# Attention's product sets: the closing product in its own PSUM bank, added by DVE, and the first feed-forward block's weights in a buffer of their own

## The chip, the core and the metric

The kernel runs on one core of a Trainium2 chip. The core has five engines that run their own instruction streams in order and meet through semaphores: TensorE (PE: matmuls, with its weight loads listed as PEld), VectorE (DVE), ScalarE (ACT), GpSimd (POOL) and SyncE (SP, which here issues nearly all DMAs). Matmul results land in PSUM, here in tiles of one bank (128 x 512 float32); everything else lives in SBUF, which DMAs fill from and store to HBM. The metric is the device time of one execution in microseconds, lower is better.

## The reference

One pre-norm transformer block over x of shape 2048 x 1024, all in float32, cut to what matters:

```python
def attn(h):                    # h = layernorm(x); 32 heads of 32
    q, k, v = (h @ w.T + b for w, b in ((wq, bq), (wk, bk), (wv, bv)))
    # per token: the 32 heads attend to one another, not to other tokens
    s = einsum('bshd,bstd->bsht', q, k) / sqrt(32)
    return einsum('bsht,bstd->bshd', softmax(s), v)

def ffn(h):                     # h = layernorm(x); 2752 hidden units
    dq1, dq2, dq3 = (nf4_quant_dequant(w) for w in (w1, w2, w3))
    return (silu(h @ dq1.T) * (h @ dq2.T)) @ dq3.T

x = x + attn(layernorm(x))
x = x + ffn(layernorm(x))
```

`nf4_quant_dequant` takes blocks of 64 weights, divides each by its largest magnitude, replaces every value by the nearest of 16 codes and multiplies back. The kernel does this on the chip, so each weight matrix has to pass through DVE and ACT before it can be used.

## The kernel before, in words

**Products.** Large matrix products are done by a Strassen-Winograd scheme: two 2 x 2 block matrices are multiplied with 7 block products in place of 8. For attention, a *product set* takes a pair of 128-token tiles (the four quadrants A11, A12, A21, A22 of their transposed activations and the sums S1 to S4) against a 1024 x 1024 projection held in SBUF as blocks B11, B21, B22 and differences T1 to T4. `products` (L314 to L358) issues the seven: SA11·B11, S3·T3, S2·T2, SA12·B21, S1·T1, S4·B22, SA22·T4, each four matmuls of 128 x 128 by 128 x 512 (`mm4`; the profile shows each as two instructions, hence x8 a product). They accumulate in place: bank `z` takes B11, T2, T1 and B22 one after the other, and ACT copies its value out in between (`g0`, `u2`, `u4`, L329) before PE may add the next; bank `q` takes T3 and T4; SA12·B21 has a bank `r` from a rotating pair (tag `x`), which also serves transposes of background weights (`ptw`) and of normalized rows (`pt` in `keep_T`). The four quadrants of the result are put together in `ce` and `co`: three by DVE adds (L346, L350, L356), the last by an ACT copy of `z` after S4·B22 (L353).

**Sweeps.** There are three sweeps of eight sets: q, k and v (in this order). Between products `products` calls `fill(n)`, n naming the product that follows in the author's count: 7, 6, 2, 5, 3, 4. A sweep's `fill` puts other work there:
- q: PE transposes of the next pair's normalized rows (`Inputs.transposes`), which ACT copies into `A` and, for v, into `V`; DVE then makes S1 to S4 (`differences`) and stores them for later sweeps.
- k: `part()`, a half of one tile's scores on PE (128 small matmuls by the profile's count), whose softmax is done by DVE and ACT. The scores of a tile take a PSUM tile `at` of four banks, of which there is one.
- v: `part()`, a half of one tile's context; DVE then transposes it (L620), adds the residual, stores it (`x1d`) and normalizes the row in place. `keep_T` transposes normalized rows on PE and stores them, and for every second tile makes four differences `xU` on DVE and stores those, as operands of the feed-forward products.

**Background.** All along, a generator `background` quantizes the feed-forward weights, 65 jobs in a fixed order. A job is an absmax, 15 steps (ACT scales into `sg`, L211, of which there are two buffers; DVE clamps and accumulates into `r`, L216) and a rescale. `advance(n)` issues n such steps; `flush(n)` moves the finished job's PE transposes (`ptw`) and ACT copies on. In the sweeps `fill` calls both; in the feed-forward loop `spent(us)` calls `advance` at 0.67 steps per microsecond of PE work issued.

**Order.** PE's instructions stand in the order in which the source issues them. Those of the other engines are placed by a scheduler that knows their dependences, so a step on DVE or a DMA on SP can stand earlier or later than its source line; on the chip each engine then runs its list strictly in order.

**First block.** After the v sweep the pools of the sweeps are closed. `plain_block` (L764) multiplies the first chunk of feed-forward weights without the Winograd scheme, eight products of four matmuls, with the last halves of context and `keep_T` in between. Its weights come by `load_w12(0, plain=True)` (L732), into a tile of the pool `wT`, which takes the SBUF space of the closed pool `pair`. Then units of seven products (`Unit`) and down projections (`down`) follow to the end: the feed-forward loop.

Of the kernel before, what the change touches and what calls it, by code (L numbers as in the profile page):

```python
# [58 lines left out]
def preln_block_kernel(  # L59
# [192 lines left out]
    wpool = ctx.enter_context(tc.tile_pool(name="op", bufs=1, side="left"))  # L252
    pair = left.enter_context(tc.tile_pool(name="pair", bufs=1, side="left"))
# [5 lines left out]
    SA11, SA12, SA22, S1, S2, S3, S4, SA21 = range(8)  # L259
# [60 lines left out]
    def products(A, fill, used=lambda name: None):  # L320
# [13 lines left out]
        g0 = copied("g0", z)  # L334
        q = ps_pj.tile([P, TB], FP, tag="q", name="q")
# [12 lines left out]
        mul(z, S1, "T1", False, False)  # L348
# [3 lines left out]
        mul(z, S4, "B22", False, True)  # L352
        nc.scalar.copy(ce[:, 512:], z)  # L353
# [6 lines left out]
    def differences(t):  # L360

        nc.vector.tensor_tensor(t[:, S1], t[:, SA21], t[:, SA22], ALU.add)
        nc.vector.tensor_tensor(t[:, S2], t[:, S1], t[:, SA11], ALU.subtract)
        nc.vector.tensor_tensor(t[:, S3], t[:, SA11], t[:, SA21], ALU.subtract)  # L364
        nc.vector.tensor_tensor(t[:, S4], t[:, SA12], t[:, S2], ALU.subtract)
# [60 lines left out]
    class Inputs:  # L426
# [3 lines left out]
        def __init__(self, p):  # L430
            self.p = p
            self.xn = [normed_x(2 * p + j) for j in range(2)]
            self.A = pair.tile([P, 8, 4, P], FP, tag="A", name="A", bufs=2)
            self.V = work.tile([P, 8, 4, P], FP, tag="AV", name="AV")

        def transposes(self, j):
            for half in range(2):
                pt = ps_t.tile([P, 4, P], FP, tag="pt", name="pt")
                for k in range(4):
                    nc.tensor.transpose(pt[:, k, :], self.xn[j][:, ts(4 * half + k, P)], ident)  # L440
                n = (SA11, SA12, SA21, SA22)[2 * j + half]
                nc.scalar.copy(self.A[:, n], pt)
                nc.scalar.copy(
                    self.V[:, n].rearrange("p k (c m) -> p k c m", c=4),
# [3 lines left out]
        def finished(self):  # L448
            differences(self.A)
            nc.sync.dma_start(opD[self.p], self.A[:, 0:7])  # L450

        def finished_v(self):
            differences(self.V)
            nc.sync.dma_start(opV[self.p], self.V[:, 0:7])
# [39 lines left out]
    def load_A(src, p):  # L494
        t = pair.tile([P, 8, 4, P], FP, tag="A", name="A", bufs=2)
        nc.sync.dma_start(t[:, 0:7], src[p])
        return t

    for p in range(NP):
# [7 lines left out]
        def fill(n):  # L507
            if n in (7, 3):
# [82 lines left out]
    for p in range(NP):  # L591
# [3 lines left out]
        def fill(n):  # L595
# [3 lines left out]
            if n in (3, 5):  # L599
# [55 lines left out]
    def keep_T(i, x1n):  # L655
# [18 lines left out]
        for n in range(4):  # L674
            u[n + 1] = work.tile([P, 4, P], FP, tag="xU", name="xU", bufs=3)
# [4 lines left out]
    for p in range(NP):  # L680
        nextA = load_A(opV, p + 1) if p + 1 < NP else None
        i = 2 * p - 4

        def fill(n):
            if n in (7, 2, 5, 4) and (p, n) != (1, 7):
                part()
            advance(2 if n == 6 else 1)
            if n in (7, 4):
                flush(1)
            if n == 5 and i in x1n:  # L690
                keep_T(i, x1n.pop(i))
            if n == 3:
                if p == 0:
                    part()
                elif i + 1 in x1n:
                    keep_T(i + 1, x1n.pop(i + 1))
# [334 lines left out]
```

## Time and profile before

| what | value |
|---|---|
| median of 3 runs | 2572.02 us (2563.67 to 2575.69) |
| profiled execution, its own time | 2561.21 us |
| profiled execution, span | 2559.4 us |
| PE busy | 2438.9 us (95%) |
| DVE busy | 2020.1 us (79%) |
| ACT busy | 1673.7 us (65%) |
| POOL busy | 31.7 us (1%) |
| mean granted PE clock | 0.985 |
| DMA | 506 MB, 198 GB/s |

Starts of product sets in the profiled execution (us): q 13.1, 44.7, 71.6, 103.3, 135.4, 166.0, 192.7, 223.8; k 250.8, 278.4, 317.0, 351.4, 381.6, 411.5, 447.2, 477.7; v 512.4, 546.2, 577.8, 610.1, 649.8, 686.6, 720.0, 757.0. The first block's products start at 801.9, the first unit's at 842.4. Sets are numbered 1 to 24 in this order.

How to read it: a busy time is that of an engine's own instructions, with neither waits nor DMA issues in it. Matmuls overlap their neighbours, so PE's busy time includes pipelining. The granted clock is what the power throttle let PE have; at 0.5 a matmul takes twice as long. Windows give these numbers for a stretch of time; waits list the idle time of an engine before an instruction, with what released it.

### The profile page before, as it was taken

How to read it: one execution, taken by the hardware profiler on the slowest of the kernel's cores; microseconds unless marked ns; L12 is line 12 of the kernel's file. 1: busy time of each engine (PE TensorE's matmuls, PEld its weight loads, DVE VectorE, ACT ScalarE, POOL GpSimd, SP SyncE). 2: the span in 40 equal slices, each digit the busy share in tenths (PEclk: the TensorE clock that was granted, in tenths of full speed). 3: DMA queues.
4: the chain of work that ended last, by engine and by line, in shares of the span. 5: the costliest groups of instructions: out<-in, count | busy, mean ns of one | idle time of the engine just before them, and what ended most of it. 6: DMA issues, size and time to landing. Idle time of an engine off the chain costs nothing.

```text
span 2559.4 us, 36651 instructions
## 1 busy us (share of the span) xinstructions
PE 2438.9 (95%) x14160; PEld 1134.1 (44%) x14160; DVE 2020.1 (79%) x2240; ACT 1673.7 (65%) x3190; POOL 31.7 (1%) x72
## 2 busy tenths in 40 slices
PE   8899899999998999999999999999999999999998
PEld 4444444444444444444444444444444444444433
DVE  8999798888998588888888888889888897871222
ACT  4656554444654478979888898888987978861000
POOL 1000000000000000000000000000000000000000
PEclk9999999999999999999999999999999999999999
DMA  8778543656668673354644547335365253641474
GB/s 301 286 281 335 210 162 121 233 189 221 224 218 290 218 271 144 136 212 138 263 155 135 198 149 265 149 118 215 128 251 192 107 205 136 234 176 70 142 279 150
DMA packets 156848, 506.03 MB, mean 198 GB/s; under 512 B 13632, under 2 KB 67904, under 8 KB 136832
## 3 DMA queue, kind: packets, MB, share of 16 engines
q1 hardware_dynamic: 156096, 503.63, 54.3%
q8 instruction: 111, 1.82, 0.3%
q14 instruction: 65, 0.53, 0.1%
q10 hardware_dynamic: 576, 0.05, 0.0%
HBM read 317.77 MB, written 185.86 MB: 197 GB/s over the span
## 4 chain that ended last, share of the span: by engine, by line
PE 22%; DVE 21%; ACT 18%; issue 6%; DMA 1%; DVEq 0%; SPq 0%
DVE r L216 17%; PE z L311 9%; PE po L929 7%; ACT sg L211 7%; ACT wn L172 6%; PE q L311 3%; ACT r L172 3%; PE rr L311 2%; ACT wop L147 1%; DVE acc L950 1%; DMA acc<-x1d 1%; PE po L941 1%; DVE r L214 1%; DVE r L227 1%; PE ptw L146 0%
## 5 line engine op out<-in xcount | busy, mean ns | idle before, releaser
L211 ACT ACTIVATE sg<-wn 128x1024 f32<-128x1024 f32 (+1 forms) x975 | 1011.0, 1047 | 318.9 <-DVE r L216 272.4
L216 DVE SCALAR_TENSOR_TENSOR r<-sg,r 128x1024 f32<-128x1024 f32 (+1 forms) x910 | 1103.1, 1212 | 111.9 <-ACT sg L211 73.9
L929 PE MATMUL po<-w,h 128*128 128x512 f32 x1344 | 595.1, 597 | 17.0 <-DVE acc L950 13.8
L929 PEld LDWEIGHTS po<-w,h 128*128 128x128 f32 x1344 | 250.0, 190 | 336.5 <-issue 286.8
L311 PE MATMUL z<-xB,w 128*128 128x512 f32 x720 | 322.7, 597 | 13.7 <-DMA w<-wd 11.3
L311 PE MATMUL z<-xT,w 128*128 128x512 f32 x656 | 297.2, 596 | 2.0 <-ACT u L861 1.9
L311 PE MATMUL q<-xT,w 128*128 128x512 f32 x656 | 291.0, 592 | 0.0
L172 ACT ACTIVATE wn<-wn,rc 128x64 f32<-128x64 f32 x1032 | 270.1, 335 | 26.4 <-DVE rc L192 26.4
L311 PEld LDWEIGHTS z<-xB,w 128*128 128x128 f32 x720 | 134.5, 191 | 174.5 <-issue 164.3
L311 PE MATMUL z<-wB,A 128*128 128x512 f32 x384 | 188.6, 637 | 22.4 <-ACT u L329 22.4
L950 DVE TENSOR_TENSOR acc<-acc,po 128x512 f32<-128x512 f32 x192 | 129.7, 681 | 101.6 <-PE po L929 58.4
L311 PEld LDWEIGHTS q<-xT,w 128*128 128x128 f32 x656 | 123.6, 190 | 151.4 <-issue 149.5
L311 PE MATMUL z<-wT,A 128*128 128x512 f32 x384 | 181.3, 616 | 8.4 <-ACT u L329 6.4
L311 PEld LDWEIGHTS z<-xT,w 128*128 128x128 f32 x656 | 122.9, 191 | 149.8 <-issue 140.7
L311 PE MATMUL q<-wT,A 128*128 128x512 f32 x384 | 173.1, 593 | 3.0 <-DVE A L364 2.0
L172 ACT ACTIVATE r<-r,am 128x64 f32<-128x64 f32 x608 | 152.4, 338 | 27.9 <-DVE r L216 27.8
L311 PE MATMUL rr<-xB,w 128*128 128x512 f32 x328 | 150.0, 600 | 0.0
L184 DVE TENSOR_REDUCE am<-wn 128x16 f32<-128x1024 f32 (+1 forms) x65 | 78.3, 1204 | 59.4 <-ACT r L172 55.5
L311 PEld LDWEIGHTS z<-wB,A 128*128 128x128 f32 x384 | 75.0, 205 | 106.5 <-issue 79.3
L311 PEld LDWEIGHTS z<-wT,A 128*128 128x128 f32 x384 | 72.1, 195 | 91.0 <-issue 81.2
L311 PEld LDWEIGHTS q<-wT,A 128*128 128x128 f32 x384 | 71.8, 190 | 90.9 <-issue 84.2
L861 ACT COPY u<-z 128x512 f32<-128x512 f32 x41 | 23.5, 573 | 131.6 <-PE z L311 131.6
(104 smaller groups left out, 1798.4 us busy)
## 6 DMA issues: line engine op xcount, KB each, us to landing
w<-wd SPq DMA_DIRECT2D x41, 1280.0 KB, 6.9
acc<-x1d SPq DMA_DIRECT2D x96, 512.0 KB, 3.8
wd<-wop SPq DMA_DIRECT2D x21, 2048.0 KB, 7.0
x1d<-acc SPq DMA_DIRECT2D x80, 512.0 KB, 2.9
wn<-in_w_dram SPq DMA_DIRECT2D x63, 512.0 KB, 4.0
w<-wd SPq DMA_DIRECT2D x62, 512.0 KB, 4.1
xT<-xdT SPq DMA_DIRECT2D x28, 1024.0 KB, 7.2
xB<-xdB SPq DMA_DIRECT2D x24, 1024.0 KB, 5.2
```

The costliest lines, as they stand in the source:

```text
L147: nc.scalar.copy(o[:q, first + half], pt[:q])
L172: nc.scalar.mul(dst[:, ts(n, BLOCK)], src[:, ts(n, BLOCK)], by[:, n : n + 1])
L184: nc.vector.tensor_reduce(am[:, :nb], v.rearrange("p (b e) -> p b e", e=BLOCK), AX.X, ALU.max, apply_absolute_value=True,)
L211: nc.scalar.activation(t, v, AF.Copy, bias=EDGES[i], scale=BIG)
L214: nc.vector.tensor_scalar(r, t, code, -1.0, ALU.min, ALU.max)
L216: nc.vector.scalar_tensor_tensor(r, t, code, r, ALU.min, ALU.max)
L227: nc.vector.tensor_tensor(r3, r3, f, ALU.mult)
L311: nc.tensor.matmul(dst, w[:, k, :], xop[:, k, :], start=start and k == 0, stop=stop and k == 3, skip_group_check=True,)
L861: nc.scalar.copy(u2, self.z)
L929: nc.tensor.matmul(po, hs[c][j][:, ts(q, P)], w3T[c][:, ts(n, 512)], start=(c == g[0]), stop=(c == g[-1]), skip_group_check=True,)
L941: nc.tensor.matmul(po, hs[NFULL][r, ts(q, P)], w3T[NFULL][r, ts(n, 512)], start=False, stop=True, skip_group_check=True,)
L950: nc.vector.tensor_tensor(a[:, ts(n, 512)], a[:, ts(n, 512)], po, ALU.add)
```

## The change

- `products`: S1·T1 now closes the accumulation in `z`. S4·B22 goes into a bank of its own, `r3`, from the rotating pair, and the last quadrant of `ce` is the DVE add of `u4` and `r3` in place of the ACT copy of `z`. There is one more call of `fill`, with n = 1, after the first product.
- `fill` in the three sweeps: the points at which `flush`, `advance`, `keep_T` and `part` run are moved; in q and k the new call issues one background step more, in v it issues none, n = 6 issues one in place of two, and three follow the set in place of two.
- The quadrant A21 leaves the tiles `A` and `V` (seven blocks of 2 KB a partition in place of eight) and gets tiles of its own for q and v; `xU` has two buffers in place of three.
- The space so freed holds a pool `w0` of 8 KB a partition, made before the sweeps' pools. The first block's weights are loaded there by an instruction that the source places at the start of the last v set, and `plain_block` is handed the tile.

```diff
--- before.py
+++ after.py
@@ -250,13 +250,15 @@
 
 
     wpool = ctx.enter_context(tc.tile_pool(name="op", bufs=1, side="left"))
+    w0p = ctx.enter_context(tc.tile_pool(name="w0", bufs=1, side="left"))
     pair = left.enter_context(tc.tile_pool(name="pair", bufs=1, side="left"))
     ps_pj = left.enter_context(tc.tile_pool(name="ps_pj", bufs=1, space=PSUM, side="left"))
     small = right.enter_context(tc.tile_pool(name="small", bufs=2, side="right"))
     ctx.enter_context(tc.manual_schedule(engines={nc.tensor.engine}))
 
     NP = NT // 2
-    SA11, SA12, SA22, S1, S2, S3, S4, SA21 = range(8)
+    SA11, SA12, SA22, S1, S2, S3, S4 = range(7)
+    SA21 = -1
     qD = [tc.dram_tile([P, 32, NH], FP, name=f"qD{i}") for i in range(NT)]
     pD = [tc.dram_tile([P, 32, NH], FP, name=f"pD{i}") for i in range(NT)]
     opD = [tc.dram_tile([P, 7, 4, P], FP, name=f"opD{p}") for p in range(NP)]
@@ -332,6 +334,7 @@
         z = ps_pj.tile([P, TB], FP, tag="z", name="z")
         mul(z, SA11, "B11", True, False)
         g0 = copied("g0", z)
+        fill(1)
         q = ps_pj.tile([P, TB], FP, tag="q", name="q")
         mul(q, S3, "T3", True, False)
         s7 = copied("s7", q)
@@ -345,23 +348,24 @@
         co = pair.tile([P, E], FP, tag="C1", name="co")
         nc.vector.tensor_tensor(ce[:, 0:512], g0, r, ALU.add)
         fill(2)
-        mul(z, S1, "T1", False, False)
+        mul(z, S1, "T1", False, True)
         u4 = copied("u4", z)
         nc.vector.tensor_tensor(co[:, 512:], u4, s7, ALU.add)
         fill(5)
-        mul(z, S4, "B22", False, True)
-        nc.scalar.copy(ce[:, 512:], z)
+        r = bank("r3")
+        mul(r, S4, "B22", True, True)
+        nc.vector.tensor_tensor(ce[:, 512:], u4, r, ALU.add)
         fill(3)
         mul(q, SA22, "T4", False, True)
         nc.vector.tensor_tensor(co[:, 0:512], u2, q, ALU.add)
         fill(4)
         return ce, co
 
-    def differences(t):
-
-        nc.vector.tensor_tensor(t[:, S1], t[:, SA21], t[:, SA22], ALU.add)
+    def differences(t, a21):
+
+        nc.vector.tensor_tensor(t[:, S1], a21, t[:, SA22], ALU.add)
         nc.vector.tensor_tensor(t[:, S2], t[:, S1], t[:, SA11], ALU.subtract)
-        nc.vector.tensor_tensor(t[:, S3], t[:, SA11], t[:, SA21], ALU.subtract)
+        nc.vector.tensor_tensor(t[:, S3], t[:, SA11], a21, ALU.subtract)
         nc.vector.tensor_tensor(t[:, S4], t[:, SA12], t[:, S2], ALU.subtract)
 
     def qk_T(t, c, b):
@@ -430,8 +434,10 @@
         def __init__(self, p):
             self.p = p
             self.xn = [normed_x(2 * p + j) for j in range(2)]
-            self.A = pair.tile([P, 8, 4, P], FP, tag="A", name="A", bufs=2)
-            self.V = work.tile([P, 8, 4, P], FP, tag="AV", name="AV")
+            self.A = pair.tile([P, 7, 4, P], FP, tag="A", name="A", bufs=2)
+            self.V = work.tile([P, 7, 4, P], FP, tag="AV", name="AV")
+            self.a21 = work.tile([P, 4, P], FP, tag="A21", name="A21")
+            self.v21 = work.tile([P, 4, P], FP, tag="V21", name="V21")
 
         def transposes(self, j):
             for half in range(2):
@@ -439,19 +445,20 @@
                 for k in range(4):
                     nc.tensor.transpose(pt[:, k, :], self.xn[j][:, ts(4 * half + k, P)], ident)
                 n = (SA11, SA12, SA21, SA22)[2 * j + half]
-                nc.scalar.copy(self.A[:, n], pt)
+                a, v = (self.a21, self.v21) if n == SA21 else (self.A[:, n], self.V[:, n])
+                nc.scalar.copy(a, pt)
                 nc.scalar.copy(
-                    self.V[:, n].rearrange("p k (c m) -> p k c m", c=4),
+                    v.rearrange("p k (c m) -> p k c m", c=4),
                     pt.rearrange("p k (m c) -> p k c m", c=4),
                 )
 
         def finished(self):
-            differences(self.A)
-            nc.sync.dma_start(opD[self.p], self.A[:, 0:7])
+            differences(self.A, self.a21)
+            nc.sync.dma_start(opD[self.p], self.A)
 
         def finished_v(self):
-            differences(self.V)
-            nc.sync.dma_start(opV[self.p], self.V[:, 0:7])
+            differences(self.V, self.v21)
+            nc.sync.dma_start(opV[self.p], self.V)
 
     load_x(0)
     load_x(1)
@@ -492,8 +499,8 @@
         return lambda name: load_W(m, name)
 
     def load_A(src, p):
-        t = pair.tile([P, 8, 4, P], FP, tag="A", name="A", bufs=2)
-        nc.sync.dma_start(t[:, 0:7], src[p])
+        t = pair.tile([P, 7, 4, P], FP, tag="A", name="A", bufs=2)
+        nc.sync.dma_start(t, src[p])
         return t
 
     for p in range(NP):
@@ -505,7 +512,7 @@
             nxt = Inputs(p + 1)
 
         def fill(n):
-            if n in (7, 3):
+            if n in (1, 6):
                 flush(1)
             if n == 5 and more:
                 nxt.transposes(0)
@@ -596,7 +603,7 @@
             if n in (7, 2, 5, 4):
                 part()
             advance(1)
-            if n in (3, 5):
+            if n in (1, 6):
                 flush(1)
 
         cs = products(A, fill, (lambda name: None) if p + 1 < NP else next_W("v"))
@@ -672,28 +679,33 @@
         b12, b22 = t[:, 0], t[:, 1]
         u = {}
         for n in range(4):
-            u[n + 1] = work.tile([P, 4, P], FP, tag="xU", name="xU", bufs=3)
+            u[n + 1] = work.tile([P, 4, P], FP, tag="xU", name="xU", bufs=2)
             y, z = ((b12, b11), (b22, u.get(1)), (b22, b12), (b21, u.get(2)))[n]
             nc.vector.tensor_tensor(u[n + 1], y, z, ALU.subtract)
             nc.sync.dma_start(xd[f"T{n + 1}", tbp][:, :, cols], u[n + 1])
 
     for p in range(NP):
-        nextA = load_A(opV, p + 1) if p + 1 < NP else None
+        if p + 1 < NP:
+            nextA = load_A(opV, p + 1)
+        else:
+
+            until("2", 0)
+            nextA = w0p.tile([P, 4, 4, P], FP, tag="w0", name="w0")
+            nc.sync.dma_start(nextA, wd["2", 0][:, 0:4])
         i = 2 * p - 4
 
         def fill(n):
             if n in (7, 2, 5, 4) and (p, n) != (1, 7):
                 part()
-            advance(2 if n == 6 else 1)
-            if n in (7, 4):
+            advance(0 if n == 1 else 1)
+            if n in (1, 2):
                 flush(1)
-            if n == 5 and i in x1n:
+            if n == 7 and i in x1n:
                 keep_T(i, x1n.pop(i))
-            if n == 3:
-                if p == 0:
-                    part()
-                elif i + 1 in x1n:
-                    keep_T(i + 1, x1n.pop(i + 1))
+            if n == 3 and p == 0:
+                part()
+            if n == 4 and i + 1 in x1n:
+                keep_T(i + 1, x1n.pop(i + 1))
 
         cs = products(A, fill, (lambda name: None) if p + 1 < NP else next_op)
         flush(1)
@@ -708,7 +720,7 @@
             t = work.tile([P, 32, D], FP, tag="vd", name="vd", bufs=3)
             v_T(t, cs[j], vb_sb)
             parts.append(gather(2 * p + j, pl[j], t))
-        advance(2)
+        advance(3)
         A = nextA
     hook["scale"] = "DVE"
     left.close()
@@ -729,14 +741,11 @@
             load_op(name, tbp)
         return ops[tag][2]
 
-    def load_w12(c, plain=False):
+    def load_w12(c):
         until("2", c)
         t = wT.tile([P, 7, 4, P], FP, tag="w12", name="w12")
-        if plain:
-            nc.sync.dma_start(t[:, 0:4], wd["2", c][:, 0:4])
-        else:
-            nc.sync.dma_start(t[:, 0:2], wd["2", c][:, 0:2])
-            nc.sync.dma_start(t[:, 2:7], wd["2", c][:, 3:8])
+        nc.sync.dma_start(t[:, 0:2], wd["2", c][:, 0:2])
+        nc.sync.dma_start(t[:, 2:7], wd["2", c][:, 3:8])
         return t
 
     def load_w3(c):
@@ -761,9 +770,8 @@
     def new_h():
         return hp.tile([P, TB], FP, tag="h", name="h", bufs=10)
 
-    def plain_block(c, tbp):
-
-        w = load_w12(c, plain=True)
+    def plain_block(w, tbp):
+
         hs = []
         for j in range(2):
             zs = []
@@ -789,7 +797,7 @@
 
 
 
-    plain = plain_block(0, 0)
+    plain = plain_block(A, 0)
     i = NT - 4
     next(plain)
     next(plain)
```

## The prediction

> **What bounds the kernel now.** I read the page's engine totals first, then one row for each stage, single product sets, then who waits for whom, and last the timeline at the places of the edits. Windows: stretch, length, then PE, PEld, DVE, ACT and POOL busy, PE's granted clock, DMA share, GB/s. The rows are the q sweep, the k sweep, seven v sets, the eighth v set with the first feed-forward block, and the feed-forward loop:
>
> ```profile
> 13.10:250.80 237.70, 217.12 (x585) 101.64 (x585) 222.89 (x281) 143.28 (x292) 16.44 (x28) 0.97 0.80 300
> 250.80:512.40 261.60, 241.58 (x4059) 120.68 (x4057) 225.15 (x221) 133.29 (x250) 0.00 (x0) 0.97 0.50 186
> 512.40:757.00 244.60, 226.20 (x3963) 117.72 (x3960) 216.85 (x227) 133.07 (x271) 8.16 (x22) 0.97 0.62 209
> 757.00:842.40 85.40, 72.91 (x1340) 39.39 (x1329) 69.12 (x77) 35.30 (x69) 4.56 (x10) 0.94 0.83 278
> 842.40:2559.40 1717.00, 1673.90 (x4202) 747.93 (x4200) 1281.66 (x1429) 1225.12 (x2305) 0.00 (x0) 0.99 0.49 179
> ```
>
> From 842 on PE is busy 1674 of 1717 us at clock 0.99: that loop is PE's. Before it (829 us) PE and DVE share the work nearly evenly, and which one ends a set changes from set to set. Four whole sets, k 14 and 15, v 22 and 23:
>
> ```profile
> 411.50:447.20 35.70, 31.26 (x581) 15.63 (x569) 35.08 (x33) 21.02 (x35) 0.00 (x0) 0.95 0.37 130
> 447.20:477.70 30.50, 30.50 (x581) 15.72 (x577) 23.16 (x26) 10.89 (x26) 0.00 (x0) 1.00 0.34 129
> 686.60:720.00 33.40, 32.43 (x604) 17.54 (x594) 25.99 (x31) 13.70 (x43) 1.48 (x4) 1.00 0.72 238
> 720.00:757.00 37.00, 33.30 (x586) 17.14 (x584) 35.61 (x36) 24.42 (x42) 1.49 (x4) 0.95 0.59 197
> ```
>
> The quantization job of the background moves in lumps: a set that holds 11 to 15 of its steps (L216) is full on DVE and lasts 35 to 37 us with PE at clock 0.95; a set with 1 is PE's, 30.5 us in k and 33.4 us in v, while DVE idles 7 us. ACT is half idle throughout, so what ACT loses is worth nothing by itself. Who waits in these 829 us (total, times, longest), and the places:
>
> ```profile
> ACT sg L211 <- DVE r L216: 113.4, 123, 6.1
> PE z L311 <- ACT u L329: 28.8, 14, 4.3
> PE z L311 <- DMA w<-wd: 11.3, 1, 11.3
> PE sc L390 <- DVE kd L382: 5.6, 1, 5.6
> ...
> 746.18 5.40 PE L311 MATMUL z<-wB,A 128*128 128x512 f32 x8 [2.96 <-ACT u L329]
> ...
> 752.29 3.60 PE L311 MATMUL q<-wT,A 128*128 128x512 f32 x8
> ...
> 801.88 8.89 PE L311 MATMUL z<-xB,w 128*128 128x512 f32 x16 [11.30 <-DMA w<-wd]
> ```
>
> `z<-wB` after an ACT wait is the closing product S4·B22, held by the copy of u4 out of the same bank. The copy is late because ACT's queue stands behind `sg`, which waits for DVE: the wait is DVE's in the end.
>
> **Part 1, the bank of its own.** Of the 28.8 us, 22.4 stand in the row of `z<-wB`: 2.8, 2.7 and 1.8 in q, 3.3 at k's first set, 4.3, 2.9 and 3.0 in v, the rest below 1. The stall also costs clock: 5.40 us where a product takes 3.60, so 1.8 more at five of them. Gross 22.4 + 5 x 1.8 = 31 us of PE time. *Trainium skill, "TensorE: Matmul & The Clock Gate", Part 1: the clock falls after an idle window of about 3.4 us. By that the 2.96 us stall would cost no clock and the gross would be 22 us; the row shows that it does cost it, so I keep 31.*
>
> Against it: the ACT copy of `ce` (0.59 us, 24 times) becomes a DVE add. Its nearest row is L346, 0.68 us, the same shapes with one side in PSUM; but what DVE pays is the distance from start to start:
>
> ```profile
> 758.48 0.70 DVE L677 TENSOR_TENSOR xU<-xT 128x512 f32<-128x512 f32 x1
> 759.08 0.69 DVE L356 TENSOR_TENSOR co<-u,q 128x512 f32<-128x512 f32 x1
> ...
> 734.45 1.21 DVE L216 SCALAR_TENSOR_TENSOR r<-sg,r 128x1024 f32<-128x1024 f32 x1
> 735.58 1.20 DVE L624 TENSOR_TENSOR x<-x,cx 128x1024 f32<-128x1024 f32 x1
> ```
>
> 0.60 us an add, 1.13 us a background step. So +4.8 us of DVE in each sweep. *"Perfetto Trace Analysis", Optimizing Scalar/DVE Operations, says to hand work from a saturated DVE to Scalar; this edit does the reverse. By it all 14.4 us would be paid; by the rows only those in sets that DVE ends.* In the new DVE order the add stands after the next context's transpose and residual add (3.0 us), which fits under the closing product (3.4 us), so the bank comes free in time for the transposes that reuse it; if DVE is over 5 us late, PE waits there instead.
>
> **Part 2, the calls of `fill`.** There are seven now. q and k issue one step more a set; v still nine. Counted in the built order of DVE, steps done at the end of q, k, v and at the second h of the first block: 58, 119, 180, 195 before; 59, 134, 195, 208 after. So q +1, k +14, v 0, block -2. They leave the feed-forward loop, where PE ends everything, for sweeps where DVE often does.
>
> *q.* DVE 222.9 of 237.7: its bound. +1 x 1.13 + 4.8 = 5.9 us; the three stalls removed let DVE's idle time shrink by at most what stands beside them (0.75, 0.75, 1.9 = 3.4). Bounds 0 to +6, taken +2.5.
>
> *k.* 14 x 1.13 + 4.8 = 20.6 us. Cover: set 10 (278 to 317), where DVE idles 12.0 us, in two waits of 3.9 and 5.3, while PE waits for `kd`; in the new order 18 steps stand there, not 4. That leaves 8.6. The three light sets with idle DVE (3.9, 7.9, 7.1) could take it, but the new order keeps lumps of 14, 1, 12, 3, 14, so I give them half: +4. The stalls of the other k sets stand at the scores (`sc`), whose single PSUM tile waits for softmax on DVE, and stay. Bounds -3 (all hidden, and the 3.3 us stall gone) to +12 (only the idle of set 10 used).
>
> *v.* The new order has 9 and 6 steps in turn in place of 14, 1, 15. At 34.3 us of DVE work (its instructions by the distances above) and 33.4 us, PE's pace in the row of set 22, I take 35 and 33.4: sets 20 to 23 last 136.8, not 147.0 (39.7 + 36.9 + 33.4 + 37.0): -10. Set 24 had no step and gets nine: +3.5. Sets 17 to 19 keep a lump of 15: 0. Sum -6.5, taken -7 for the clock. `xU` has two buffers, not three: the third difference now waits for the store of the first (median 4.3 us from issue to landing) with 0.6 to 2 us of other work between; some 2.3 us of DVE a set, hidden in the 6-step sets, and queued behind it is the transpose that frees the context tile for PE. Bounds -18 (all at PE's pace) to +4.
>
> **Part 3, the weights of the first block.** No wait holds the new load, and in SP's built order it stands back in the q sweep, so the 11.3 us and 8.89 - 6.9 = 2 us of clock go. What is late next is DVE. It had covered that wait with 14 steps (795 to 814); these now lie among the block's residual chains. From the last `co` add to the last normalized row DVE has 38 us of work by the same distances, plus about 4 us for the third `xU` (four differences in a row) and 4 to 5 for `h`, which waits for PE's fourth half-product: 47 to 48 us against 51.5 (790.1 to 841.6). -3; bounds -12 (PE alone: its products, contexts and transposes take 40.5) to +5.
>
> **Feed-forward.** Both orders start a new job after the first unit's h, the new one a job ahead. Nothing is gained while PE ends the loop; but three transposes waited 11.7 us for jobs, with slow clock after (some 6.8 us more). A job ahead may remove one or shift them: -10 to +5, taken -3.
>
> **Sum.** 2.5 + 4 - 7 - 3 - 3 = -6.5 us on the profiled execution: span 2559.4, time 2561.2, to 2555. The median of the runs lies 10.8 above it, 2572.0; I give 2565.
>
> **Rivals.** *A, DVE pays (slower):* the new order holds 27.8 us more DVE work before the loop (5.9 + 20.6 + 4.8, less the block's 2 steps and smaller moves). If DVE's idle time doesn't shrink except in set 10 (12 us), 16 are paid, and with `xU` holding v at its old pace the block's gain is lost: 2588. For it: heavy sets idle DVE under 1.5 us; against: the v lumps go. It decides once the even v sets last 36 us or more. *B, PE's pace is reached (faster):* v -18, block -8, loop -8, q and k 0: 2538. For it: 31 + 13 us of PE stalls go; against: DVE set most of them. *C, the load was hidden anyway:* DVE's steps under the wait were work that had to be done, the block keeps its 51.5 us and the waits move to context and h: 2572 with part 1's small sums.
>
> **How the numbers follow.** 0.5%, 12.9 us, is about what a measurement of this kernel can tell from no change. The forecast with C (2559 to 2580): 0.40; B and what lies towards it: 0.34; A: 0.26. A few of the first group's cases fall past the near bound, so faster 0.38, same 0.34, slower 0.28. The forecast's own range is 2553 to 2580; with both rivals cut at one in ten, 2540 to 2591.
>
> **What would show it.** Right: no PE wait for `u` before a closing product; v sets 20 to 23 at 33 to 36 us; k longer by a few us; no wait on the load, with PE's next waits at context on the transpose behind `xU`. Wrong: v sets still at 37 (A), or the stretch from 13 to the first unit shorter by over 20 us (B).

## The result, and the profile after

The changed kernel takes 2591.02 us (median of 4 runs, 2588.82 to 2595.1) against 2570.73 us before (4 runs on the same chip, 2563.67 to 2575.69). The ratio is 1.0087, with a 95% interval of 1.0069 to 1.0106: slower by 20 us, where 7 us faster was forecast. The profiled execution went from 2561.21 to 2591.23 us, its span from 2559.4 to 2589.4. That is 30 us, since the profiled execution of before lies 9.5 below the median beside it and that of the changed kernel 0.2 above its own. So the stages below add up to 10 us more than the medians differ by.

The windows of the changed kernel, stage by stage as before (q, k, seven v sets, the eighth with the first block, the loop), and then v sets 20 to 23. Columns: stretch, length, busy time of PE, PEld, DVE, ACT and POOL, PE's granted clock, DMA share, GB/s:

```profile
12.69:248.70 236.01, 214.31 (x586) 99.99 (x585) 225.52 (x288) 138.87 (x285) 13.72 (x28) 0.98 0.80 300
248.70:524.10 275.40, 246.44 (x4065) 123.07 (x4063) 250.54 (x249) 151.09 (x291) 0.00 (x0) 0.94 0.51 188
524.10:770.70 246.60, 225.19 (x3972) 117.07 (x3961) 209.21 (x221) 116.46 (x238) 11.33 (x20) 0.97 0.60 204
770.70:867.90 97.20, 77.97 (x1331) 42.49 (x1330) 79.37 (x88) 42.44 (x70) 7.95 (x12) 0.90 0.79 266
867.90:2589.40 1721.50, 1676.91 (x4193) 747.56 (x4192) 1266.22 (x1414) 1207.76 (x2280) 0.00 (x0) 1.00 0.49 176
624.20:664.30 40.10, 33.76 (x587) 17.36 (x586) 35.74 (x40) 18.15 (x37) 3.44 (x5) 0.91 0.66 205
664.30:697.90 33.60, 32.38 (x594) 17.27 (x593) 26.51 (x29) 14.60 (x30) 1.48 (x4) 1.00 0.69 229
697.90:736.10 38.20, 33.38 (x587) 17.21 (x586) 33.84 (x39) 17.80 (x36) 3.04 (x5) 0.96 0.64 201
736.10:770.70 34.60, 32.45 (x594) 17.33 (x593) 27.02 (x29) 15.00 (x32) 1.90 (x4) 1.00 0.62 214
```

Against the rows of before: q 1.7 us shorter, k 13.8 longer, the seven v sets 2.0 longer, the last set with the block 11.8 longer, the loop 4.5 longer. DVE's work ahead of the loop rose from 734.0 to 764.6 us (the sum of its four rows), and the loop starts 25.5 us later. The loop got 15.4 us less of DVE work and no shorter for it. In set 22 DVE has 33.8 us of work, as the prediction counted (34.3), yet the set lasts 38.2 and DVE idles 4.4 of them. So its pace is not DVE's alone.

Who waits, in the first 870 us of the changed kernel (total, times, longest):

```profile
ACT xT L669 <- DVE xU L684: 23.2, 7, 6.6
PE r L313 <- ACT xT L669: 19.3, 5, 6.3
DVE xU L684 <- DMA xdT<-xU: 16.0, 6, 6.2
...
PE sc L394 <- DMA ql<-qD: 11.9, 1, 11.9
...
PE ptw L146 <- ACT r L172: 8.2, 1, 8.2
...
PE pt L668 <- DVE x L308: 6.3, 1, 6.3
...
PE z L313 <- ACT u L331: 3.8, 5, 1.5
```

PE's wait for `u` fell from 28.8 us to 3.8, and the 11.3 us for the first block's weights are gone. In their place PE waits 19.3 us for a bank that ACT has to empty into `xT` first. The timeline of set 22 (start, length, engine and line, what ended the idle time before it) shows who holds whom:

```profile
706.11 1.09 PE L668 MATMUL pt<-ident,x 128*128 128x128 f32 x8
707.03 3.60 PE L313 MATMUL z<-wT,A 128*128 128x512 f32 x8
...
712.29 1.92 DVE L627 STREAM_TRANSPOSE cx<-cx 128x1024 f32<-128x1024 f32 x1
714.07 0.67 DVE L684 TENSOR_TENSOR xU<-xT,xU 128x512 f32<-128x512 f32 x1
...
714.81 1.07 ACT L669 COPY xT<-pt 128x512 f32<-128x512 f32 x2 [1.35 <-DVE xU L684]
...
715.45 5.40 PE L313 MATMUL r<-wB,A 128*128 128x512 f32 x8 [4.82 <-ACT xT L669]
```

`keep_T`, moved to n = 7, transposes into the rotating pair at 706.1. The product that takes the pair next is not the closing S4·B22 but SA12·B21, one product later. ACT may not copy `pt` into `xT` until DVE has made the last difference `xU` that reads the old `xT`, and that stands behind steps and a context transpose. PE idles 4.82 us, and SA12·B21 then takes 5.40 us in place of 3.60. The same wait stands in sets 20 and 24 (6.34 and 4.78 us).

### The profile page after: what moved, and what is told of

Same layout as the page of the kernel before. It is cut to its first block, busy times and chain, and to the rows that moved or that the text cites. A ratio compares the mean times of both kernels' runs of the same rounds, so it can differ in the third digit from the quotient of the medians.

```text
span 2589.4 us, 36654 instructions
## 1 busy us (share of the span) xinstructions
PE 2447.9 (95%) x14160; PEld 1136.9 (44%) x14160; DVE 2035.3 (79%) x2264; ACT 1660.2 (64%) x3166; POOL 35.5 (1%) x72
## 4 chain that ended last, share of the span: by engine, by line
DVE 23%; ACT 21%; PE 16%; issue 7%; DMA 2%; DVEq 0%; SPq 0%
DVE r L216 18%; ACT sg L211 8%; ACT wn L172 6%; PE po L937 6%; PE z L313 5%; ACT r L172 4%; PE q L313 3%; ACT wop L147 1%; PE rr L313 1%; DVE acc L958 1%; DVE am L184 1%; DVE r L227 0%; DVE r L214 0%; ACT g L873 0%; DMA acc<-x1d 0%
## 5 line engine op out<-in xcount | busy, mean ns | idle before, releaser
L313 PE MATMUL r<-wB,A 128*128 128x512 f32 x384 | 188.1, 636 | 19.3 <-ACT xT L669 19.3
L147 ACT COPY wop<-ptw 128x512 f32<-128x512 f32 (+1 forms) x130 | 74.6, 574 | 77.1 <-PE ptw L146 77.0
L313 PEld LDWEIGHTS r<-wB,A 128*128 128x128 f32 x384 | 75.7, 204 | 109.9 <-issue 85.0
```

The source lines that it names most:

```text
L147: nc.scalar.copy(o[:q, first + half], pt[:q])
L313: nc.tensor.matmul(dst, w[:, k, :], xop[:, k, :], start=start and k == 0, stop=stop and k == 3, skip_group_check=True,)
```

## The experiments

The differences below are between ratios to the kernel before, in units of 2572 us; their margins join the two runs' intervals. First the kernel was cut into its parts.

**Part 3 alone.** The kernel before with the `w0` pool, A21 in tiles of its own, `xU` with two buffers; products and `fill` as before.

```diff
+    w0p = ctx.enter_context(tc.tile_pool(name="w0", bufs=1, side="left"))
...
+            nextA = w0p.tile([P, 4, 4, P], FP, tag="w0", name="w0")
+            nc.sync.dma_start(nextA, wd["2", 0][:, 0:4])
```

> The kernel before with part 3 alone: the first block's weights in a buffer of their own, A21 in tiles of its own, two xU buffers; products, fill and steps as before. Forecast's step for part 3 (-3 us): ratio 0.997 to 1.000, the wait of 11.3 us gone. Theory X (two buffers cost more than the wait gave): the block's waits on the xU stores come with it, ratio 1.000 to 1.005. Theory S says only that it is not slower: 0.995 to 1.000.

2562.23 us, 0.9965 (0.9953 to 0.9977): 9 us faster than before. The window of its last v set and first block, 97.2 us in the changed kernel:

```profile
761.60:844.70 83.10, 75.07 (x1340) 40.51 (x1329) 68.55 (x77) 34.87 (x68) 4.70 (x10) 0.94 0.88 294
```

The row of before had 85.4. Its profiled execution (2565.9) lies above its median, that of before below, so the rest of the 9 us cannot be placed in the two traces. What the rest of the change costs is 0.0122, 31 us. All further single edits stand on this kernel, called the base here.

**Three xU buffers on the base** (room from single `mx` and `sm` tiles of the softmax).

> The kernel before with the weights' own buffer and three xU buffers (room from single buffers for the softmax's maxima and sums). If the store of the first difference holds DVE as it does in the changed kernel: 0.993 to 0.996, 2552 to 2560 us, the eighth v set some 3 to 5 us shorter than its 34.0 or the block shorter than its 49.1. If the third buffer is worth nothing here: 0.996 to 0.998.

2562.53 us, 0.9975 (0.9961 to 0.9989): no gain.

**The bank alone, and DVE's copy alone.** The first puts S4·B22 into `r3` with DVE's add, with `fill` as before; the second keeps the product set of before and lets DVE copy `z` in ACT's place.

```diff
-        nc.scalar.copy(ce[:, 512:], z)
+        nc.vector.tensor_copy(ce[:, 512:], z)
```

> The kernel before with the weights' own buffer, and with the bank r3 and DVE's add; fill is called as before (six times, no n = 1). Theory P1: 1.005 to 1.011, 2583 to 2598 us, and PE waits some 15 us or more before S4*B22 in r for ACT's copies. Theory P2: 0.990 to 0.998, 2545 to 2565 us: the 22 us of waits for u before the closing product go and nothing takes their place. If the two parts only cost together (the moved transposes of keep_T meet the shared bank): both this run and the one with fill alone below 1.000.

> The kernel before with the weights' own buffer, and the copy of z after S4*B22 on DVE instead of ACT: 24 more DVE instructions of about 0.6 us, 14.4 us, and no new bank. If DVE's share of the work is what makes the bank variant slow: 1.000 to 1.004, 2570 to 2581 us (8 to 18 us over the buffer alone at 0.9965). If DVE's idle time takes them: 0.995 to 0.998, 2557 to 2566 us; then the DVE add is no part of the loss.

2578.2 us, 1.0021 (1.0008 to 1.0035), and 2575.11 us, 1.0016 (1.0005 to 1.0027). Handing 24 instructions of 0.6 us from ACT to DVE costs 0.0051, 13 us (9 to 17), nearly all of their 14.4. The bank as a whole costs 14, 1 us more than DVE's copy alone (-3 to 6), so taking the closing product out of `z` bought nothing that can be told. PE's waits before 870 us, on the base and then with the bank on it:

```profile
PE z L313 <- ACT u L331: 27.1, 16, 4.3
```

```profile
PE r L313 <- ACT xT L668: 18.4, 5, 6.7
...
PE q L313 <- DVE co L359: 8.6, 5, 3.8
```

Here `keep_T` stands at n = 5, just ahead of S4·B22, and it is that product that waits in the rotating pair, 18.4 us. Another 8.6 us (0.3 on the base) stand before S3·T3 of the next set, whose bank `q` DVE's last add `co` still has to read. Together that is the base's 27.1 us for `u`. By stages, one execution each, the bank made q shorter (229.1 us, 233.1 on the base), k longer (276.1, 270.5) and the seven v sets, where `keep_T` runs, longer by 14 (259.7, 245.6).

**The moved calls without the bank.** The changed kernel with the product set of before, `fill(1)` kept.

> The changed kernel with the product set of before: S4*B22 accumulates in z again and ACT copies it out; the calls of fill (n = 1 among them) stay where the change put them, and so does the weights' own buffer. Reference point: the buffer alone with the fill of before measured 0.9965 of before, the whole change 1.0087, some 31 us apart. Theory P1 (the bank r3 and DVE's add cost it): 0.994 to 0.999, 2555 to 2568 us, no PE wait for xT copies before S4*B22. Theory P2 (the new fill points cost it): 1.005 to 1.011, 2583 to 2598 us, with the k sweep at 270 us or more and the eighth v set with the first block at 95 us or more. If each part costs something of its own: 0.999 to 1.005.

2589.7 us, 1.0078 (1.0059 to 1.0098): 0.0113, 29 us, over the base. This part does nearly the whole damage; the bank on top of it adds 2 us (-5 to 9), which cannot be told from nothing. Its last v set and block take 95.8 us, close to the changed kernel's 97.2; its k takes 268.0, no more than the base, with all the added steps in it.

**The moved calls one at a time, on the base.** `flush` at its new points; `keep_T` at n = 7 and 4 in v; one step more a set in q and k; v's ninth step from n = 6 to the end of the set.

```diff
+        fill(1)
...
-            if n == 5 and i in x1n:
+            if n == 7 and i in x1n:
...
-            advance(2 if n == 6 else 1)
+            advance(0 if n == 1 else 2 if n == 6 else 1)
```

> The kernel before with the weights' own buffer (0.9965 of before) and, of the moved calls, only flush: at n = 1 and 6 in q and k, at 1 and 2 in v; no step at n = 1, keep_T and the steps as before. All the moved calls together, without the bank, measured 1.0078: some 29 us. Theory F (the rotating pair is taken by a job's transposes just before SA12*B21 needs it, and jobs end at other places): 1.002 to 1.008, 2576 to 2590 us, with PE waits in the rows of r or ptw. If flush's place is worth nothing: 0.994 to 0.999, 2555 to 2568 us.

> The kernel before with the weights' own buffer and, of the moved calls, only v's keep_T, at n = 7 and 4 in place of 5 and 3. Theory K (keep_T at n = 7 puts its two pt tiles into the rotating pair one product ahead of SA12*B21, which then waits for ACT's copies, themselves held by the xU that reads the old xT): 1.001 to 1.006, 2574 to 2587 us, PE r behind xT copies 15 us or more in v, the eighth v set 5 us longer than its 34.0. If the move is harmless alone: 0.994 to 0.999.

> The kernel before with the weights' own buffer and, of the moved calls, only one background step more a set in q and k (n = 1), so that one whole job of 15 steps leaves the feed-forward loop for the sweeps. Theory S (steps are free in the loop and paid in the sweeps): 15 x 1.13 = 17 us more DVE work before the loop, 1.001 to 1.004, 2574 to 2582 us, the first unit 8 us or more later than at 844.7. If DVE's idle time takes them, as taking them out of the whole change suggested: 0.994 to 0.999.

> The kernel before with the weights' own buffer and, of the moved calls, only v's ninth step: after the set (three there) in place of a second one at n = 6. No step count changes. Theory V (where the lumps of a job fall against the sets decides it, and this moves them): more than 6 us either way from 0.9965, so under 0.994 or over 0.999. If the place of one step is worth nothing: 0.994 to 0.999.

| on the base | median us | ratio to before | against the base |
|---|---|---|---|
| flush moved | 2568.05 | 0.9989 (0.9977 to 1.0002) | +6 us (2 to 10) |
| keep_T moved | 2578.93 | 1.0032 (1.0018 to 1.0046) | +17 us (13 to 22) |
| steps added | 2587.59 | 1.0059 (1.0037 to 1.0080) | +24 us (18 to 31) |
| ninth step moved | 2563.86 | 0.9965 (0.9951 to 0.9979) | 0 us (-5 to 5) |

What `flush` costs stands in the first block. On the base the job that runs there makes its first step (L214) 4 us after the block's first product, with `flush` moved 22 us after it. The rows are the base's, then those with `flush` moved:

```profile
799.78 0.68 DVE L214 TENSOR_SCALAR r<-sg 128x1024 f32<-128x1024 f32 x1
```

```profile
812.91 0.68 DVE L214 TENSOR_SCALAR r<-sg 128x1024 f32<-128x1024 f32 x1
...
844.53 1.94 PE L667 MATMUL pt<-ident,x 128*128 128x128 f32 x8 [7.31 <-DVE x L308]
```

DVE idles early in the block, then has the steps in front of the last normalized row, and PE waits 7.31 us for that row. From its first product to the first unit the block takes 55.1 us, on the base 49.1. The other traces agree: in all nine kernels with `flush` at its new points the block takes 52.5 to 55.2 us and PE's wait for that row 5.3 to 10.5; in the ten others with the parts of the change, 45.5 to 50.0, and the wait is 3.4 at most.

With `keep_T` moved, PE waits at SA12·B21, as in the changed kernel:

```profile
PE r L313 <- ACT xT L667: 15.3, 5, 7.1
```

Added steps cost more than their DVE work (15 x 1.13 = 17 us). Set 10 shows where some of it stands. Its window in the kernel with added steps, and PE's largest wait in it:

```profile
281.60:331.10 49.50, 34.08 (x570) 16.81 (x568) 43.15 (x42) 35.90 (x76) 0.00 (x0) 0.83 0.48 178
```

```profile
PE sc L393 <- DVE kd L385: 12.4, 1, 12.4
```

The set holds 20 steps and lasts 49.5 us, where the base's has 6 and lasts 42.7. DVE's former idle time there is used, but PE stands still beside it, here until DVE has made `kd`. That wait is mostly not new. On the base PE waits 10.1 us at the same place for `ql`. So the wait accounts for some 2 of the 6.8 us.

**Steps taken out, and added elsewhere.** Without the step at n = 1 in q and k: from the whole change, and from the moved calls without the bank. The bank on the base with it. And the base with a step less a set (none at n = 6 in q and k).

```diff
-            advance(0 if n == 5 else 1)
+            advance(0 if n in (5, 1) else 1)
```

> The changed kernel, but the new call of fill issues no background step in q and k, so that these sweeps hold as many steps as in the kernel before. Theory S (steps: the k sweep's +13.9 us is DVE work of 14 background steps that the feed-forward loop did for nothing): k falls from 275 to 260-264 us, v and the first block stay at 247 and 97 +-4, the total is 10 to 16 us below the changed kernel, ratio to before 1.002 to 1.005. Theory X (the two xU buffers and the earlier keep_T hold ACT and PE in v and in the block, and k's growth is the adds' and the late ql load's): k falls by 5 us at most, ratio 1.006 to 1.009.

> The moved calls without the bank (1.0078 of before), and without their one step more a set in q and k. If the 15 steps cost their DVE work wherever they stand (theory S, 24 us when added alone): 0.997 to 1.001, 2562 to 2574 us. If only the place of the jobs' lumps counts, as taking them out of the whole change suggested (nothing came back): 1.004 to 1.009, 2580 to 2595 us, with DVE idle 10 to 20 us more than the 97.8 us before the loop.

> The weights' own buffer with the bank and DVE's add (1.0021 of before), and one step more a set in q and k; the other calls as before. Theory S: 1.009 to 1.013, 2594 to 2604 us. If the steps' work goes into DVE's idle time once the bank holds PE elsewhere: 1.000 to 1.005, 2571 to 2584 us.

> The weights' own buffer alone (0.9965 of before) with one step a set less in q (none at n = 6) and k (none at n = 6): a job of 15 steps goes from the sweeps to the feed-forward loop. Theory S, that steps are paid before the loop and free in it: 0.986 to 0.993, 2535 to 2554 us. If the place of the lumps counts and not their number: 0.994 to 1.003. If the loop then waits for its weights, its 1710 us grow by what is late.

| the step at n = 1 | with it | without | price |
|---|---|---|---|
| base | 1.0059 | 0.9965 | 24 us (18 to 31) |
| bank on the base | 1.0098 (1.0081 to 1.0115) | 1.0021 | 20 us (14 to 25) |
| moved calls, no bank | 1.0078 | 1.0045 (1.0027 to 1.0063) | 8 us (2 to 15) |
| whole change | 1.0087 | 1.0088 (1.0074 to 1.0102) | 0 us (-6 to 6) |

Taking one more step out of the base gives 2563.28 us, 0.9969 (0.9958 to 0.9981): nothing. So the same 15 steps cost between 0 and 24 us. Their number does not set the price. A fixed cost of the steps' work falls, and with it the simple form of "DVE pays". That the place of the jobs' lumps decides is argued, not shown. One run speaks against it: the ninth step, moved, took the lump of 13 steps out of set 21 and put 15 into set 22, where 2 were, and cost 0 us (-5 to 5).

The traces show where the step's price went in the whole change (one execution each). Without the step, q and k are 4.6 and 3.4 us shorter (231.4 and 272.0). But from the first v set to the first unit, where both kernels do the same 76 steps in other lumps, the one without it is 9.8 us longer. With it, then without:

```profile
524.10:867.90 343.80, 303.16 (x5301) 159.56 (x5290) 288.58 (x308) 158.90 (x307) 19.28 (x32) 0.95 0.65 221
```

```profile
515.90:869.50 353.60, 309.53 (x5297) 161.70 (x5290) 285.11 (x305) 153.70 (x282) 19.33 (x32) 0.93 0.63 214
```

In q one wait takes both the step and `flush` at its new points: PE's 8.2 us in set 3 of the changed kernel, before the transposes of a job that ACT has still to rescale. That set lasts 38.2 us there, and 27.6 to 30.2 with only the step, with only `flush` moved, or in the whole change without the step.

**keep_T and the bank.** The changed kernel with v's `keep_T` back at n = 5 and 3; and the bank on the base with `keep_T` at n = 1 and 3, away from both products that use the pair.

```diff
-            if n == 5 and i in x1n:
+            if n == 1 and i in x1n:
```

> The changed kernel with keep_T in the v sweep back at the places of the kernel before (after the fifth and the sixth product), so that the transposes no longer share the rotating banks just ahead of r. Theory X in its bank form: PE's wait for the xT copy ahead of r (19.3 us in five) vanishes, sets 20, 22 and 24 fall from 38-42 to 34-36 us, ratio 1.004 to 1.006. If the wait only moves behind the closing product, or if the xU stores alone are to blame: ratio 1.007 to 1.010. Theory S: 1.007 to 1.009.

> The weights' own buffer with the bank and DVE's add (1.0021 of before), and keep_T at n = 1 and 3 instead of 5 and 3: two products before SA12*B21, and after S4*B22; steps and flush as before, none at n = 1. If the shared pair is what gives the bank's gain back: the 18 us of waits of r for xT copies fall below 6, and with their clock 0.990 to 0.997, 2545 to 2564 us. If DVE is what ends these sets: 1.000 to 1.004, 2571 to 2582 us, and PE waits elsewhere. If keep_T at n = 1 still holds SA12*B21: as the bank with the calls of before, 1.002.

2600.44 us, 1.0118 (1.0104 to 1.0132), and 2578.08 us, 1.0033 (1.0019 to 1.0047). With `keep_T` back, the wait moves to S4·B22, and the time is 8 us (2 to 14) above the changed kernel's; moving it was right once the bank is there:

```profile
PE r L313 <- ACT xT L669: 20.9, 6, 5.1
```

With `keep_T` apart from both products, no `r` waits for `xT` any more, and the time cannot be told from that of the bank alone (3 us more, -2 to 8). PE's waits of that kernel before 870 us:

```profile
PE pt L668 <- ACT xT L669: 12.4, 2, 6.4
PE pt L668 <- DVE ce L357: 11.9, 4, 7.4
```

Now the transposes wait: 11.9 us for DVE's add to free `r3`, 12.4 for the copies of the transposes before. That the pair itself is short, so that whoever comes next in it waits, is how these runs read together; no run gave the pair a third bank.

**The buffers behind the chain.** Three `xU` buffers in the changed kernel (room again from single `mx` and `sm` tiles); the whole change with the weights loaded as before; the same with two buffers for each `xT` tile.

```diff
-            u[n + 1] = work.tile([P, 4, P], FP, tag="xU", name="xU", bufs=2)
+            u[n + 1] = work.tile([P, 4, P], FP, tag="xU", name="xU", bufs=3)
...
-        t = work.tile([P, 2, 4, P], FP, tag=f"xT{i % 2}", name="xT")
+        t = work.tile([P, 2, 4, P], FP, tag=f"xT{i % 2}", name="xT", bufs=2)
```

> The changed kernel with three xU buffers again (two small softmax tiles of the k sweep get one buffer in place of two, to make room). Theory X: the DVE waits on the xU stores (16 us in six before 870) fall below 6, the waits of ACT's xT copies on xU and of PE's closing product on xT with them, v from 512 to the first unit shortens by 8 to 16 us, ratio to before 1.003 to 1.006. Theory S: under 4 us, ratio 1.007 to 1.009.

> The whole change without the weights' own buffer: the first block's weights come by the load of before; the other tiles as in the changed kernel, so 8 KB stay free. If the buffer is worth within the change what it was worth alone (9 us): 1.010 to 1.014, 2597 to 2607 us, with a PE wait for w before the first block. If it was worth something only where PE got there early enough: 1.006 to 1.010.

> As h1, with two buffers for each of the two xT tiles. If the chain is xU on DVE reading the old xT, then ACT's copy into it, then the rotating bank, then SA12*B21: the waits of r for xT copies (19.3 us in the changed kernel) fall below 6, the v sweep is 8 us or more shorter than in h1 and the ratio 0.003 or more below h1's. If ACT's copies are late for another reason (its queue behind sg, that is DVE's load): waits stay above 12 and the ratio within 0.002 of h1's.

2589.82 us, 1.0075 (1.0062 to 1.0088); 2603.33 us, 1.0118 (1.0100 to 1.0136); 2599.11 us, 1.0106 (1.0089 to 1.0122). The weights' buffer is worth 8 us (1 to 15) within the change too. Three `xU` buffers bring 3 us (-3 to 9), two `xT` buffers 3 (-3 to 9): neither can be told from nothing. In the windows the seven v sets go from 251.8 to 248.0 us with two `xT` buffers, and PE's wait for the copies between 512 and 780 us, without and with the second buffer:

```profile
PE r L312 <- ACT xT L668: 14.1, 4, 5.7
```

```profile
PE r L312 <- ACT xT L668: 7.2, 2, 3.9
```

In these two executions half of the wait goes with the second `xT` buffer, half stays. ACT's timeline in set 20 with two `xT` buffers:

```profile
635.05 1.06 ACT L211 ACTIVATE sg<-wn 128x1024 f32<-128x1024 f32 x1 [5.92 <-DVE r L216]
...
638.54 0.57 ACT L330 COPY s<-q 128x512 f32<-128x512 f32 x1
639.31 1.06 ACT L211 ACTIVATE sg<-wn 128x1024 f32<-128x1024 f32 x1 [0.21 <-DVE r L216]
640.28 1.05 ACT L668 COPY xT<-pt 128x512 f32<-128x512 f32 x2
```

ACT had stood 5.92 us behind a step of DVE, and five instructions of its list came before the copy. Neither theory of that run holds alone.

No kernel measured is faster than the base: part 3 without parts 1 and 2, ahead of before by 0.0035 and of the whole change by 0.0122.

## Why the prediction was wrong

The time fell on the edge of the range (2591) and on the other side of the likeliest case. By its steps:

- **What bounds the kernel: held.** As soon as PE no longer waited for `u`, it waited for DVE's work at other instructions. DVE's added work ahead of the loop was put at 27.8 us and measured 30.6.
- **Part 1, the step that failed first.** "so the bank comes free in time for the transposes that reuse it" looked at one user of the rotating pair after another product, in one direction only. The wait for `u` went, as counted. But the pair also serves `keep_T`, and a product that follows `keep_T` waits for ACT and DVE to empty it: 18.4 us at S4·B22 with the old points, 19.3 at SA12·B21 with the new ones, 11.9 + 12.4 at the transposes with neither. Beside DVE's copy alone the bank gained nothing.
- **DVE's add was under-priced.** Only the adds in sets that DVE ends were to be paid, within terms of +2.5 in q and 4.8 gross in k. The copy alone measured 13 us of 14.4. The Trainium skill, "Perfetto Trace Analysis", Optimizing Scalar/DVE Operations, says that where DVE is saturated it may make sense to hand some of its work to Scalar. Here DVE was busy 222.9 of q's 237.7 us, and the price of the reverse, all 14.4, agrees with that run.
- **v, the largest miss: -7 taken, +9.1 measured, above its upper bound of 4.** The term runs over eight sets to the last `co` add, not over the seven of the rows above (512.4 to 790.1 before, 524.1 to 811.0 after). Sets 20 to 24 have 9 and 6 steps in turn, as counted, and set 22 has 33.8 us of DVE work against 34.3. Sets 21 and 23 lasted 33.6 and 34.6, near the 33.4 taken, but sets 20 and 22 lasted 40.1 and 38.2, where 35 was taken. So sets 20 to 23 gained 0.4 us, not 10. Set 24 to that add took 7.1 us more, where 3.5 was taken, and sets 17 to 19, taken at 0, hold 22 steps in place of 16 and took 2.3 more. Sets 20, 22 and 24 hold the wait for the pair, 15.9 us, and 7.1 us of clock after it. Part 2's `keep_T` brought them and the working never priced them; `keep_T` moved alone cost 17 us. Set 22's row stands above, these are those of 20 and 24:

```profile
643.23 5.82 PE L313 MATMUL r<-wB,A 128*128 128x512 f32 x8 [6.34 <-ACT xT L669]
...
788.21 6.71 PE L313 MATMUL r<-wB,A 128*128 128x512 f32 x8 [4.78 <-ACT xT L669]
```

- **k: +4 taken, +13.8 measured, above its upper bound of 12.** The cover was wrong at least in part. DVE did use set 10's idle time, but the set grew from 38.6 to 44.6 (before, then after):

```profile
278.40:317.00 38.60, 32.97 (x577) 16.78 (x576) 26.40 (x27) 17.00 (x44) 0.00 (x0) 0.91 0.50 171
```

```profile
274.40:319.00 44.60, 32.53 (x575) 16.34 (x573) 43.17 (x45) 32.38 (x63) 0.00 (x0) 0.85 0.55 195
```

  The working counted all of DVE's idle time there as cover while PE stood still beside it, waiting for `kd`. In the changed kernel the last wait in that set is for `ql` (11.9 us). The base has it too (10.1 us, in a set of 42.7 us), so most of the 6 us is neither the steps' nor the adds'. The same holds for the whole sweep: the base, with neither, took 270.5 us, and three kernels much like it there (last section) 264.7 to 267.8, that is 3 to 9 us over the 261.6 of before. Taking the steps out of the whole change gave 3.4 us back. Why k is longer without them stays open.
- **Part 3: sign right, size too small, while the block grew by part 2.** -3 was taken. Alone the weights' buffer measured -9, within the change -8. The span that the working counted, from the last `co` add to the last normalized row, was put at 47 to 48 us. It took 47.4 on the base (795.9 to 843.3), as counted, but 55.0 in the changed kernel (811.0 to 866.0), 3.5 more than before's 51.5. The working gave the new points of `flush` no price, and `flush` moved alone lengthens the block by 6 us, as in the changed kernel. Set 24 and the block in the changed kernel, then on the base:

```profile
770.70:812.60 41.90, 35.48 (x590) 18.15 (x589) 38.15 (x43) 18.49 (x35) 3.21 (x6) 0.92 0.79 277
812.60:867.90 55.30, 42.48 (x743) 24.34 (x742) 41.22 (x46) 23.95 (x35) 4.74 (x6) 0.89 0.80 258
```

```profile
761.60:795.60 34.00, 32.43 (x604) 17.51 (x593) 24.40 (x29) 8.91 (x26) 1.48 (x4) 1.00 0.95 323
795.60:844.70 49.10, 42.64 (x738) 23.00 (x737) 44.15 (x49) 25.96 (x43) 3.22 (x6) 0.90 0.83 274
```

  Set 24's 7.9 us are the wait at SA12·B21 (4.78 us) and the clock after it (3.1). In the block the third and fourth `xU`, put at 4 us, waited 8.1 (1.93 and 6.17) for stores. That wait alone does not set the block's length: with three `xU` buffers in the changed kernel the stores hold DVE 1.8 us there, and the block still takes 54.7.
- **The loop: -3 taken, +4.5 measured,** within its bounds: no gain from a job ahead shows where PE ends the work. The base, without it, took 2.4 more than before.
- **The rivals.** A named the time (2588) and its deciding point came true: the even v sets lasted over 36 us. Its mechanism was half of it, so that its number fits is partly luck. DVE paid for the copy (13 us) but the same steps cost 0 to 24 us depending on what stood beside them, and in the long v sets DVE idled over 4 us. B needed PE's stalls to vanish; they moved. C fell: the weights' buffer is worth its 9 us.

The single prices on the base, 14 + 6 + 17 + 24, make 61 us, and all together cost 31. So they overlap; which wait hides which was not shown. Why the added steps cost 24 us on the base, and in the whole change gain in v what they lose in q and k, stays open.

## What to carry to other kernels

A product given a bank of its own inherits every other user of that bank: list who fills and who empties each rotating buffer, in both directions, and price the slowest emptier before counting the old stall as a gain. Idle time of an engine is no safe cover where another engine stands still beside it: in set 10 all of it was counted, and the set still grew. A call that is moved needs a price of its own, also in a later stage: here `flush` moved in the sweeps put a job's steps in front of the first block's last row. A change in several parts should be run part by part: here the part that looked like a side effect was the gain, and the moved calls were most of the loss.

## What was not expected of the hardware

A short stall is followed by half clock at one time and not at another (a matmul of the `r` products in that trace takes 0.59 us, at most 1.22). Three waits before S4·B22 in the changed kernel with `keep_T` back at its old points:

```profile
612.23 5.31 PE L313 MATMUL r<-wB,A 128*128 128x512 f32 x8 [1.92 <-ACT xT L669]
...
689.39 5.40 PE L313 MATMUL r<-wB,A 128*128 128x512 f32 x8 [2.01 <-ACT xT L669]
...
766.79 3.70 PE L313 MATMUL r<-wB,A 128*128 128x512 f32 x8 [1.92 <-ACT xT L669]
```

The first two cost 1.6 to 1.7 us of clock on top, the third nothing. Before has a longer one that cost nothing, at k's first set:

```profile
271.43 3.70 PE L311 MATMUL z<-wB,A 128*128 128x512 f32 x8 [3.27 <-ACT u L329]
```

The length of the one stall does not tell which. The prediction's 1.8 us at five of before's stalls was read from the rows; as a price for stalls to come it is an average at best.

The length of one stage differs between executions by more than one might read from it. The base and the two kernels with the same source in q and k (`keep_T` moved, the ninth step moved) took 270.5, 264.7 and 267.4 us in k, and the one with three `xU` buffers, whose softmax has single `mx` and `sm` tiles, 267.8. So of the k term's 13.8 us some 3 either way may be chance of one execution, while the ratios above come from 4 to 12 executions of each kernel.
